# Fewer slots for the tiles of a two-layer graph network, another last pair of tiles in layer 2, and another cut of the last softmax

## The chip, the cores and the metric

The kernel runs on one core of one Trainium2 chip. A core has five engines that run their own instruction queues side by side: TensorE (PE; its weight loads are shown apart as PEld), VectorE (DVE), ScalarE (ACT), GpSimd (POOL) and SyncE (SP). Transfers between the chip's memory (DRAM) and the on-chip buffer are made by DMA engines; indirect ones, which pick rows by a list of indices, are issued by POOL, most others by SP. The metric is the device time of one execution in microseconds (us), lower is better; the number that stands for a kernel is the median of its runs.

## The reference

10,000 nodes with 768 numbers each pass through two graph attention layers with residuals. The graph has 80,000 random edges in both directions and a self loop for each node, sorted by destination; the layer adds another self loop. Cut to what matters:

```python
def gat_conv(x, edge_index, W, a_src, a_dst, bias, heads, out_ch, concat):
    xl = (x @ W).reshape(n, heads, out_ch)
    alpha_src = jnp.einsum('nhc,hc->nh', xl, a_src)
    alpha_dst = jnp.einsum('nhc,hc->nh', xl, a_dst)
    e = jax.nn.leaky_relu(alpha_src[src] + alpha_dst[dst], 0.2)
    e = jnp.exp(e - segment_max(e, dst)[dst])
    alpha = e / (segment_sum(e, dst)[dst] + 1e-16)
    out = segment_sum(xl[src] * alpha[:, :, None], dst)
    return out + bias

h = relu(layer_norm(gat_conv(x, ..., heads=4, out_ch=256))) + (x @ Wr1 + br1)
y = layer_norm(gat_conv(h, ..., heads=1, out_ch=768)) + (h @ Wr2 + br2)
return _layernorm(x + y)
```

For each node, the rows of its some 17 neighbours are fetched, weighted by a softmax over them, and added.

## The kernel before

**Sorting.** While the products `x @ W1` are made tile by tile and written to a table in DRAM (`table1`, 1033 numbers a node), `prepare` counts the neighbours of each node on the device, sorts the nodes by that count, most first, and writes for each node the list of its neighbours (`slots`). 128 nodes of the sorted order make a tile, 79 in all; a node of a tile stands on one of the 128 partitions. A tile's number of slots is the same for its 128 nodes and has to be known when the program is built. `slot_counts` (line 60 on) works it out: it takes the degree as Poisson distributed, and for tile t it looks for the smallest k for which the expected number of nodes with more than k neighbours, and a room of some standard deviations above it, is no more than t x 128. The counts of before, by sorted tile, run from 41, 27, 26, 25, 24, 24, 23 down to 11, 10, 9, 8, 1377 in all. Unused slots name a row of the table beyond the nodes, whose logit is -1e30. A comparison on the device (`fits`) sends the program to `general_path`, without slots, if a node has more neighbours than its tile has slots.

**Layer 1** (`ordered_layer1`) visits the tiles in the order `TURNS`: every second one from the smallest up to the one of 41 slots, then the others from 27 down. For each slot POOL issues one indirect DMA (`Ring.fetch`, issued by `gather`, L426) that brings one row for each of the 128 nodes into a ring of 31 slots; after the first 31, indices out of range are skipped and move nothing. ScalarE multiplies rows by their weights (L516), VectorE or PE adds them up (L523, L527, L728), and PE makes the products for the residual (L173) and for layer 2's table (L904). Near the start of the work on a tile, ScalarE copies the table row of two tiles earlier in two parts (L829).

**Layer 2** (`ordered_layer2`) fetches rows of 770 numbers into a ring of 41 slots; a tile's first slot, the nodes' own rows, is brought by SP (L455), the others by POOL, and unused slots fetch the row beyond the nodes. A slot's next row is asked for right after VectorE's step for the old one is issued, and POOL waits until VectorE and PE have both read the old one. The order of its tiles, `turns`, is made before it (line 641 on): the three smallest tiles in front, two held back for the end (`final`), and the rest mixed so that the running mean of the slots stays near the mean of all, taking the largest or the smallest of those left. For a tile t the loop issues, in this order:

- on PE the residual of tile t+1 (L1061, L1064: 34 recorded matmuls),
- on VectorE the first norm step of tile t-1: statistics of its two parts in the accumulator and of its part in PSUM (L538), then ScalarE's standard deviation (L542, L543),
- a row at a time, columns 0 to 511 on VectorE (L527), with three further norm steps of tile t-1 between the rows (L552, L554, L1074, L538, then ScalarE's L1080 and POOL's store L1082),
- from a slot called `turn` on, the logits and the softmax of tile t+1 (L489 to L507), its diagonals on ScalarE (L1018), and columns 512 to 767 of its rows on PE (L1019).

A tile of 26 slots or more (`PARTED2`: those of 41, 27 and 26) takes its softmax in two parts, with cuts from `cuts_of`: the second part's logits come three slots before the cut, its weights and PE's share one slot before it, and the sums so far are scaled by `fade`.

Of the kernel before, what the change touches and what calls it, by code (L numbers as in the profile page):

```python
# [42 lines left out]
DEGREES = 64  # L43
# [10 lines left out]
PARTED2 = 26  # L54
# [9 lines left out]
def slot_counts(n_nodes, n_edges):  # L64

    rate = max(n_edges / n_nodes - 1.0, 0.1)
    tails, term, below = [], math.exp(-rate), 0.0
    for k in range(DEGREES):
        below += term
        tails.append(max(n_nodes * (1.0 - below), 0.0))  # L70
        term *= rate / (k + 1)
    counts = []
    for t in range(-(-n_nodes // P)):
        room = t * P if t else 0.002
        k = next((k for k, m in enumerate(tails)
                  if m + 4.0 * math.sqrt(m * (1.0 - m / n_nodes)) * (t > 0) <= room), DEGREES - 3)
        counts.append(min(k + 1, DEGREES - 2))
    return counts

# [2 lines left out]
def gnn_kernel(ctx, tc, x, x_cols, src, dst, src_col, dst_col, W1, a_src1, a_dst1, b1, g1, be1, Wr1, br1,  # L82
# [9 lines left out]
    NT = -(-N // P)  # L92
    NP = NT * P
    NCH = src_col.shape[1]
    NA = dst.shape[0] // (P * P)
    CAPS = slot_counts(N, n_edges)
    SLOTS = CAPS

# [469 lines left out]
    with tc.tile_pool(name="w1", bufs=1) as w1p, tc.tile_pool(name="l1", bufs=2) as io, \  # L568
# [51 lines left out]
        for t in range(NT):  # L620
# [3 lines left out]
            for i, vec in enumerate((ad_b, as_b)):  # L624
                m = io.tile([P, C1], F32, name="scr")
# [13 lines left out]
    SLOTS, FIRST = [SLOTS[t] for t in TURNS], [FIRST[t] for t in TURNS]  # L639
    SLOTS1, FIRST1 = SLOTS, FIRST  # L640
    turns = sorted(range(NT), key=lambda t: SLOTS[t] + 2 * (t >= NT - 2))
    first, left, final = turns[:3], turns[5:], turns[3:5]
    mean, mixed = sum(SLOTS[t] for t in left) / len(left), []
    while left:
        few = sum(SLOTS[t] for t in mixed) <= mean * len(mixed)
# [1 line left out]
    turns = first + mixed + final  # L647
# [314 lines left out]
    def ordered_layer2(mem, begun):  # L962
# [4 lines left out]
        with tc.tile_pool(name="b2", bufs=1) as pool, tc.tile_pool(name="small2", bufs=2) as small, \  # L967
# [33 lines left out]
            def cuts_of(t):  # L1001

                n = SLOTS[t]
                return [0, n // 2, n] if n >= PARTED2 else [0, n]

            def weights_of(t):


                n, at, cuts = SLOTS[t], FIRST[t], cuts_of(t)
                ad = small.tile([P, H2], F32, name="ad")  # L1010
                nc.vector.tensor_add(ad, ring.slot(at)[:, C2:C2 + H2], lift)
# [83 lines left out]
            for t in range(NT):  # L1095
                n = SLOTS[t]
# [3 lines left out]
                if not ready:  # L1100
                    ahead = weights_of(t)
                    ready += itertools.islice(ahead, 2)
                es, later, cuts = dict(ready[0]), ahead, cuts_of(t)
                acc = ps_acc.tile([P, BANK], F32, name="acc")
                if not t:
# [3 lines left out]
                if t + 1 < NT:  # L1109

                    ahead = weights_of(t + 1)
                    turn = min(max(n // 3, cuts[-2] + 1, n + cuts_of(t + 1)[1] + 4 * LEAD - ring.size), n - LEAD)
# [305 lines left out]
```

## Time and profile before

| | us |
|---|---|
| median of 3 runs | 5525.66 |
| lowest and highest of them | 5516.87, 5533.84 |
| the profiled execution | 5484.34 |
| its span, first to last instruction | 5482.5 |
| mean granted TensorE clock in it | 0.944 |

In the profile, lines such as `L527 DVE SCALAR_TENSOR_TENSOR acc<-ring,e,acc` name the line of the kernel, the engine, the operation, what is written and what is read. A view by stretches gives, for each stretch of the span, its length, the busy time of each engine with the number of its instructions, the granted clock, the mean share of time in which the DMA engines were busy, and GB/s. Two groups of the page that make up most of POOL's and VectorE's work:

```profile
L426 POOL DMA_INDIRECT ring<-table,slots x2675 | 2661.1, 995 | 1515.9 <-issue 641.3
L527 DVE SCALAR_TENSOR_TENSOR acc<-ring,e,acc 128x256 f32<-128x256 f32 (+1 forms) x2574 | 1600.5, 622 | 161.4 <-PE acc L728 72.5
```

After the bar stand the busy time in us, the mean ns of one, the idle time of the engine just before such instructions, and what ended most of it.

### The profile page before, as it was taken

To read this page: it belongs to the slowest core of one execution; us is meant where nothing else is said; L and a number is where in the kernel's file an instruction comes from. 1 tells how busy PE (TensorE), PEld (TensorE's weight loads), DVE (VectorE), ACT (ScalarE), POOL (GpSimd) and SP (SyncE) were. 2 spreads that over 40 slices of the span, in tenths; PEclk is the share of its full clock that TensorE was granted. 3 is DMA by queue.
4 is the path that set the end of the run, shared out by engine and by line. 5 is a ranking of instruction groups with operands and counts; after the bars stand their busy time and mean duration, and the time that the engine had idled before them with its cause. 6 is when DMAs were issued, how large, how long until landed. Compare 5 with 4: busy or idle time off the path is not lost. (4 is left out here: it accounts for less than half of the span.)

```text
span 5482.5 us, 58273 instructions
## 1 busy us (share of the span) xinstructions
PE 4905.3 (89%) x14359; PEld 2707.8 (49%) x14359; DVE 4205.0 (77%) x7341; ACT 2959.9 (54%) x8299; POOL 3341.8 (61%) x3659
## 2 busy tenths in 40 slices
PE   8999995999999987899999997888888888888887
PEld 3444442555544443444445554555555555555554
DVE  5783343889988888888899995777777777777876
ACT  3434443778889988889888872222222222222322
POOL 2446455566667766677676644666666666666663
PEclk9999997999999998999999999989999998988898
DMA  4333636899999998999999977988898898888984
GB/s 156 121 101 90 92 94 216 312 340 363 366 369 377 379 351 291 348 360 384 372 370 363 351 268 261 327 315 309 311 323 313 305 318 304 300 300 301 315 307 168
DMA packets 474303, 1591.30 MB, mean 290 GB/s; under 512 B 118327, under 2 KB 122487, under 8 KB 473958
## 3 DMA queue, kind: packets, MB, share of 16 engines
q0 software_dynamic: 322384, 1286.62, 65.0%
q1 hardware_dynamic: 149520, 297.43, 16.2%
q10 hardware_dynamic: 2054, 3.42, 0.2%
q8 instruction: 122, 2.00, 0.1%
q14 instruction: 223, 1.83, 0.1%
HBM read 1431.80 MB, written 177.29 MB: 293 GB/s over the span
## 5 line engine op out<-in xcount | busy, mean ns | idle before, releaser
L426 POOL DMA_INDIRECT ring<-table,slots x2675 | 2661.1, 995 | 1515.9 <-issue 641.3
L516 ACT ACTIVATE ring<-ring,e 128x256 f32<-128x256 f32 x4232 | 1740.4, 507 | 87.3 <-DVE e L773 49.3
L527 DVE SCALAR_TENSOR_TENSOR acc<-ring,e,acc 128x256 f32<-128x256 f32 (+1 forms) x2574 | 1600.5, 622 | 161.4 <-PE acc L728 72.5
L523 DVE TENSOR_TENSOR acc<-acc,ring 128x1024 f32<-128x1024 f32 x781 | 961.7, 1231 | 66.9 <-ACT ring L516 12.0
L1064 PE MATMUL big<-wr,w 128*128 128x512 f32 (+1 forms) x2464 | 874.6, 499 | 129.8 <-issue 128.0
L1019 PE MATMUL big<-ring,diagonals 128*128 128x256 f32 x2754 | 743.7, 427 | 184.1 <-issue 151.2
L173 PE MATMUL big<-w,xT 128*128 128x512 f32 x1896 | 824.0, 596 | 23.0 <-DMA w<-in_W_dram 10.1
L904 PE MATMUL half<-w,hT 128*128 128x512 f32 (+1 forms) x2528 | 830.4, 486 | 0.0
L173 PE MATMUL big<-wr,xT 128*128 128x512 f32 x1896 | 830.0, 594 | 0.2 <-ACT xT L699 0.2
L1018 ACT ACTIVATE diagonals<-ident,e 128x128 f32<-128x128 f32 x1377 | 422.9, 390 | 641.9 <-PE big L1019 176.2
L1019 PEld LDWEIGHTS big<-ring,diagonals 128*128 128x128 f32 x2754 | 585.6, 216 | 343.2 <-issue 230.4
L1064 PEld LDWEIGHTS big<-wr,w 128*128 128x128 f32 x2464 | 479.9, 196 | 495.6 <-issue 465.8
L904 PEld LDWEIGHTS half<-w,hT 128*128 128x128 f32 x2528 | 477.7, 189 | 372.8 <-issue 331.7
L728 PE MATMUL acc<-ring,ident 128*128 128x512 f32 x1108 | 522.2, 618 | 107.9 <-ACT ring L516 59.8
L173 PEld LDWEIGHTS big<-w,xT 128*128 128x128 f32 x1896 | 361.4, 191 | 481.1 <-issue 463.0
L173 PEld LDWEIGHTS big<-wr,xT 128*128 128x128 f32 x1896 | 355.4, 191 | 418.2 <-issue 417.6
L542 ACT ACTIVATE sd<-mv,eps 128x1 f32<-128x1 f32 x237 | 70.0, 296 | 748.6 <-DVE mv L540 314.6
L728 PEld LDWEIGHTS acc<-ring,ident 128*128 128x128 f32 x1108 | 212.9, 196 | 372.0 <-issue 208.4
L626 DVE TENSOR_TENSOR scr<-big,ad_b 128x1024 f32<-128x1024 f32 x79 | 96.7, 1225 | 374.7 <-ACT row L623 350.9
L631 POOL TENSOR_TENSOR row<-row,none 128x1024 f32<-128x1024 f32 x79 | 187.2, 2370 | 261.4 <-ACT row L623 259.5
L629 ACT ACTIVATE scr<-scr 128x256 f32<-128x256 f32 x632 | 254.5, 404 | 120.3 <-DVE scr L626 120.3
L623 ACT COPY row<-big 128x1024 f32<-128x1024 f32 x79 | 79.7, 1009 | 312.8 <-issue 283.6
(193 smaller groups left out, 3392.8 us busy)
## 6 DMA issues: line engine op xcount, KB each, us to landing
ring<-table,slots POOLq DMA_INDIRECT x2675
table<-row SPq DMA_DIRECT2D x79, 516.0 KB
h_d<-hT SPq DMA_DIRECT2D x79, 512.0 KB
w<-h_d SPq DMA_DIRECT2D x77, 512.0 KB
table<-row SPq DMA_DIRECT2D x79, 385.0 KB
ring<-table SPq DMA_DIRECT2D x79, 385.0 KB
xT<-in_x_cols_dram SPq DMA_DIRECT2D x79, 384.0 KB
x_d<-xt SPq DMA_DIRECT2D x79, 384.0 KB
```

Source lines behind the costliest of these rows:

```text
L173: nc.tensor.matmul(p[:, c:e], aT[:, j, :], w[:, j, c:e], start=(j == 0), stop=(j == k - 1))
L426: nc.gpsimd.indirect_dma_start(out=to, out_offset=None, in_=table, in_offset=bass.IndirectOffsetOnAxis(ap=index, axis=0), **more)
L516: nc.scalar.activation(row[:, s], row[:, s], AF.Copy, scale=e[:, h:h + 1])
L523: nc.vector.tensor_add(acc[:, :c], acc[:, :c], row[:, :c])
L527: nc.vector.scalar_tensor_tensor(acc[:, s], row[:, s], e[:, h:h + 1], (acc if first is None else first)[:, s], op0=OP.mult, op1=OP.add)
L629: nc.scalar.activation(m[:, s], m[:, s], AF.Copy, accum_out=row[:, C1 + i * H1 + h:C1 + i * H1 + h + 1])
L631: nc.gpsimd.tensor_add(row[:, :C1], row[:, :C1], b1_b)
L728: nc.tensor.matmul(acc[:, c:c + BANK], ident, ring.slot(q + k)[:, c:c + BANK], start=(k == 0), stop=(k == m - 1))
L904: nc.tensor.matmul(q, hT[:, j, :], w2[:, j, c:c + q.shape[1]], start=(j == 0), stop=(j == K1 - 1))
L1018: nc.scalar.activation(diagonals[:, (k - lo) % G, :], ident, AF.Copy, scale=e[:, k - lo, :])
L1019: nc.tensor.matmul(to, diagonals[:, (k - lo) % G, :], ring.slot(at + k)[:, ON_PE2:C2], start=False, stop=(k == n - 1), skip_group_check=True)
L1064: nc.tensor.matmul(r[:, c:d], hT[:, j, :], wr2[:, j, c:d], start=False, stop=(j == K1 - 1 and d < C2), skip_group_check=True)
```

## The change

```diff
@@ slot_counts
     for t in range(-(-n_nodes // P)):
         room = t * P if t else 0.002
         k = next((k for k, m in enumerate(tails)
-                  if m + 4.0 * math.sqrt(m * (1.0 - m / n_nodes)) * (t > 0) <= room), DEGREES - 3)
+                  if m + 3.0 * math.sqrt(m * (1.0 - m / n_nodes)) * (t > 0) <= room), DEGREES - 3)
         counts.append(min(k + 1, DEGREES - 2))
@@ the order of layer 2
     turns = sorted(range(NT), key=lambda t: SLOTS[t] + 2 * (t >= NT - 2))
-    first, left, final = turns[:3], turns[5:], turns[3:5]
+    first, left, final = turns[:3], turns[3:-3] + turns[-1:], turns[-3:-1]
     mean, mixed = sum(SLOTS[t] for t in left) / len(left), []
@@ cuts_of in ordered_layer2
                 n = SLOTS[t]
-                return [0, n // 2, n] if n >= PARTED2 else [0, n]
+                return [0, n - 8 if t == NT - 1 else n // 2, n] if n >= PARTED2 else [0, n]
```

Six tiles lose one slot, by sorted place: 28 (19 to 18), 43 (17 to 16), 58 (15 to 14), 64 (14 to 13), 69 (13 to 12) and 78 (8 to 7); in layer 1's order these are the tiles 25, 61, 10, 7, 74 and 0, counted from 0. The sum is 1371. In layer 2 the tiles held back are no longer those of 11 and 9 slots but those of 26 and 27; the order becomes 7, 10, 11, 41, 11, 9, 12, 12, 25, 12, 24, 12, 13, 24, 13, 23 and so on, to 17, 18, 17, 26, 27. Before it was 8, 10, 11, 41, 12, 12, 12, 13, 13, 27, 13, 26, 13, 13, 25, 11, 24 and so on, to 18, 18, 18, 11, 9. The last tile, now of 27 slots, is cut at 19; those of 41 and 26 are still cut in the middle.

## The prediction

> **What bounds the kernel now.** I read the page first, for the share of each engine; then a view that cuts layer 2 into stretches; then the waits of VectorE in the longest of them.
>
> ```profile
> span 5482.5 us, 58273 instructions
> PE 4905.3 (89%) x14359; PEld 2707.8 (49%) x14359; DVE 4205.0 (77%) x7341; ACT 2959.9 (54%) x8299; POOL 3341.8 (61%) x3659
> PEclk9999997999999998999999999989999998988898
> DMA  4333636899999998999999977988898898888984
> POOL out_dram L1082 0%; POOLq L1365 0%
> ```
>
> The page's chain breaks off at the last store, so it names nothing; the stages have to be read one by one. The first six slices are the products and the sorting, which the change leaves alone. Slices 7 to 24 are layer 1 (DMA 9), the rest is layer 2, where nothing is full and the granted clock falls. The stretches (us, then the busy time of PE, PEld, DVE, ACT, POOL, each with its instruction count, clock, DMA share, GB/s) begin and end at VectorE's statistics of the previous tile's PSUM part (L538), the first thing it does for a new tile:
>
> ```profile
> 3382.60:3488.80 106.20, 77.20 (x252) 51.26 (x251) 69.42 (x140) 26.54 (x85) 71.26 (x75) 0.85 0.90 309
> 3488.80:3573.10 84.30, 77.64 (x257) 49.88 (x257) 80.13 (x171) 30.16 (x93) 55.45 (x59) 0.93 0.93 336
> 3573.10:5413.40 1840.30, 1545.75 (x4986) 1015.12 (x4984) 1373.72 (x2734) 521.09 (x1618) 1171.87 (x1212) 0.89 0.88 309
> 5413.40:5482.50 69.10, 43.81 (x161) 29.85 (x161) 52.70 (x104) 15.13 (x44) 3.98 (x4) 0.84 0.12 44
> ```
>
> The first row is the tiles of 8, 10, 11 and 41 rows. The second, which I call the small stretch, is five tiles of 12 and 13 rows: VectorE works 80.1 of 84.3 us. The third, the middle, is 67 tiles with 1207 rows: VectorE works 1373.7 of 1840.3 and waits 466.6 us, 7.0 a tile. The fourth, the tail, is the tiles of 18, 11 and 9 rows and the end; no gather is left in it. What VectorE waits for in the middle:
>
> ```profile
> DVE st L538 <- PE big L1064: 124.1, 15, 15.2
> DVE w L554 <- ACT sd L543: 105.5, 10, 12.0
> DVE st L538 <- remote: 99.4, 12, 11.9
> DVE w L554 <- ACT sd L542: 29.9, 3, 12.9
> ```
>
> Nearly all of it stands at the two norm steps of a tile, behind PE (in the code's order, ScalarE's standard deviation is queued behind diagonals whose buffers PE must free). So layer 2 lasts as long as VectorE's work and these waits, and the question is what the change does to each.
>
> **Rows left out, layer 1.** With the smaller room the counts at six sorted places fall by one: 19 to 18, 17 to 16, 15 to 14, 14 to 13, 13 to 12, 8 to 7; 1377 rows become 1371. In layer 1 those rows are empty slots, whose gather is told to skip out-of-range rows, so they may carry no bytes while the DMA share is 0.92 to 1.00. What a row is worth is read from tiles of equal size, by the two copies that each tile's table row takes (L829; time, busy time, copies):
>
> ```profile
> 1046.80:1097.00 50.20, 1.89 (x4) 1.00 0.92 335
> 1097.00:1175.90 78.90, 2.83 (x6) 1.00 0.92 339
> 1174.70:1285.30 110.60, 3.48 (x8) 1.00 0.94 350
> 1514.10:1603.70 89.60, 2.51 (x6) 1.00 0.98 370
> 1603.70:1634.90 31.20, 0.83 (x2) 1.00 0.98 365
> 1634.90:1728.60 93.70, 2.51 (x6) 1.00 0.99 375
> 2772.90:2886.50 113.60, 3.34 (x8) 1.00 1.00 376
> 2886.50:2967.60 81.10, 2.52 (x6) 1.00 0.98 365
> 3151.60:3225.40 73.80, 2.84 (x6) 1.00 0.94 341
> 3225.40:3248.70 23.30, 0.94 (x2) 1.00 0.94 336
> ```
>
> Per tile: 13 rows 25.1, 14 rows 26.3, 15 rows 27.65; 18 rows 29.9, 19 rows 31.2; coming down, 17 rows 28.4, 16 rows 27.0, 13 rows 24.6, 12 rows 23.3. The fifth row is the very tile of 19 whose last slot is empty: it took 31.2, as did its three neighbours with full slots. So the empty row is paid like a full one, and the time goes with the instructions. Prices: 1.2 + 1.35 + 1.3 + 1.4 + 1.3 = 6.55. The first tile saves one gather before work begins:
>
> ```profile
> 5408.63 0.95 POOL L426 DMA_INDIRECT ring<-table,slots  x1 [0.30 <-DMA ring<-table,slots]
> 5409.88 0.95 POOL L426 DMA_INDIRECT ring<-table,slots  x1 [0.31 <-issue]
> ```
>
> 0.95 + 0.30 = 1.25 us. Layer 1 gives 7.8; the lower bound is 0, if the DMA share sets the pace after all. The sorting before it issues the same instructions with lists one entry shorter: nothing. In layer 2 the first tile saves another 1.25.
>
> **Rows left out and order, layer 2.** The old order opens with 8, 10, 11, 41, then 12, 12, 12, 13, 13, and ends 18, 11, 9. The new one opens 7, 10, 11, 41, then 11, 9, 12, 12, and ends 17, 26, 27. The small stretch falls from five tiles (62 rows) to four (44). A row costs VectorE 28.35 / 38 = 0.75 us (fourth row below), so a tile with 11 instead of 12.4 rows takes 16.86 - 1.05 = 15.8, and four take 63.3: **21.0 us less**.
>
> The middle gets 69 tiles with 1205 rows in place of 67 with 1207: 26, 27 and the 13s beside them go, 34.9 rows stand in a pair of neighbours where 36.0 stood. How a pair's time goes with its rows (time, L527 busy, rows, then clock and DMA):
>
> ```profile
> 3748.60:3801.90 53.30, 26.19 (x35) 0.90 0.89 316
> 3801.90:3858.40 56.50, 28.46 (x38) 0.88 0.85 302
> 4026.20:4192.30 166.10, 83.22 (x111) 0.91 0.91 316
> 5413.40:5482.50 69.10, 28.35 (x38) 0.84 0.12 44
> 4470.90:4800.90 330.00, 161.70 (x216) 0.88 0.89 308
> 4890.60:5221.00 330.40, 161.70 (x216) 0.89 0.89 306
> 5244.70:5413.40 168.70, 80.86 (x108) 0.89 0.87 303
> ```
>
> These are pairs of 11/24, 14/24, 22/15 (three), 20/16 (six), 17/19 (six) and 18/18 (three). Two readings. By rate: the new middle has 490 rows in uneven pairs, at (53.3 + 56.5 + 166.1) / 184 = 1.50 a row; 261 in pairs like 20/15 at 330.0 / 216 = 1.53; 454 in near-equal pairs at (330.4 + 168.7) / 324 = 1.54: 735 + 399 + 699 = 1833. By slope: a pair of 38 took 3.2 more than one of 35, 1.07 a row; a tile with 0.55 fewer rows costs 27.47 - 0.59 = 26.88, times 69 = 1855. I take **1840, no change**, nearer the rates, since they are measured on pairs of the new shapes.
>
> The tail now holds 53 rows where the ring has 41 slots. The last gather goes out after row 11 of the tile of 26, so until then the pace is that of the middle; afterwards VectorE runs alone. Both tiles stand in the middle now, with the end in the third row:
>
> ```profile
> 3573.10:3611.90 38.80, 36.33 (x125) 24.06 (x123) 29.55 (x64) 11.29 (x36) 25.48 (x27) 0.96 0.87 309
> 3640.70:3672.30 31.60, 31.60 (x118) 22.93 (x118) 28.73 (x62) 10.65 (x35) 20.16 (x21) 0.94 0.86 302
> 5463.30:5482.50 19.20, 0.00 (x0) 0.00 (x0) 5.17 (x11) 2.03 (x5) 0.98 (x1) 0.50 0.10 39
> ```
>
> The tile of 26 is taken at its 31.6. The tile of 27 is taken at its VectorE work, 29.55, because its wait of 38.8 - 29.55 came with 24 gathers beside it and there will be none. With the end, 80.35 against 69.1: **11.2 us more**. If the 27 keeps its 38.8, 20.5 more.
>
> The last tile is cut at 19 rows and not at 13. Its second softmax is computed 8 rows before the end, when the last gather has long landed, so no queue waits on it; PE's last 8 rows run beside VectorE's 8 x 0.75 = 6.0. I cost this at nothing. On SP the moved tiles' own rows and residual loads are issued at the same places of the loop, two tiles ahead; POOL's queue loses 12 gathers in all and keeps its 79 stores.
>
> A rule that speaks against the small last part:
>
> ```profile
> 5390.75 10.33 PE L1019 MATMUL big<-ring,diagonals 128*128 128x256 f32 x36
> 5415.68 8.04 PE L1019 MATMUL big<-ring,diagonals 128*128 128x256 f32 x36
> ```
>
> The same 36 matmuls took 10.33 us just after a pause and 8.04 in an unbroken run. The Trainium skill, "TensorE: Matmul & The Clock Gate", section "Part 1: The HAM clock gate", says that PE runs at half clock after an idle window and needs some 3.4 us of work to get back; the two rows agree in sign. By it the sixteen matmuls of the last part, after PE's pause in the first part of the tile, would run at twice 8.04 / 36, 16 x 0.45 = 7.1, and VectorE would wait 1 us: the sum would be 18 and not 19.
>
> **The sum.** -7.8 - 1.25 - 21.0 + 0 + 11.2 = **-18.9 us** of the profiled execution's 5484.34 (span 5482.5 and 1.8 around it): 5465.4, or 0.34% less. The runs' median is 5525.66, 41 above that execution, so I carry the share over: 5525.66 x 0.9966 = 5507.
>
> **The rivals.** *The wait belongs to the boundary, not to the row.* VectorE's 7.0 us a tile then comes 69 times in the middle and not 67, +14, and its work there grows by 6 (two more tiles' fixed steps at 7 each, less the 7.8 that the split softmaxes of 26 and 27 take away): middle 1860, and the sum is +1, 5527. For it: the wait stands at the two norm steps, once a tile each. Against it: in the small stretch the boundary waits next to nothing.
>
> *Slower: the whole tile time is fixed in the middle.* Gathers, PE's signals and the norm run round a ring of 41 slots; pairs of 36, 37 and 38 rows took 55.0, 55.4 and 56.5, so perhaps a tile costs 27.47 whatever its size. Then 69 tiles take 1895, +55, and the sum is +36: 5562. It decides as soon as the middle's mean passes 27.2 us a tile (1876 in all). For it, that flat row; against, the pair of 35 at 53.3 and the 16.9 of the small tiles.
>
> *More than forecast.* If the wait falls with the rows of a pair in a straight line from 1.7 at 25 rows (small stretch) to 13.9 at 36, a pair of 34.9 waits 12.7; the middle is 1380 + 438 = 1818 and the sum is -41: 5484.
>
> *The change doesn't do what it says:* if one node has more neighbours than the smaller room, the kernel takes its general path, which this trace doesn't price and which would lie far above any range here. Counted from the reference's own inputs, the largest degrees of the six smaller tiles are 18, 16, 14, 13, 12 and 6, so each still fits, five without a slot to spare.
>
> **How the numbers follow.** The forecast with its stronger form has 0.50 (0.42 and 0.08), the boundary rival 0.31, the slower one 0.18, the general path 0.01. A measurement of this kernel tells about 0.3%, 16.6 us, from no change. So faster 0.50, within 0.30, slower 0.20. The forecast's own range is 5497 to 5521: the middle at 1833 gives -26, and layer 1 at nothing gives -11, with the middle at 1855 +4 (taken half-way, -4). The whole range goes from 5477, the stronger form less the 9 us by which the fastest run of before lay under its median, to 5546, half-way from the boundary rival to the slower one.
>
> **What would show it.** Right: layer 1's tiles at the five places shorter by 1.2 to 1.4; a small stretch near 63 after the tile of 41; 69 tiles in about 1840 us with VectorE waiting under 7 us each; about 80 us from the start of the tile of 26. Wrong: a middle above 1876, or the tile of 27 waiting at L538 for PE with no gather in flight, or at L489 for its last rows. If the middle is right and the time isn't, the tail is the next place to look; if layer 1's tiles don't shorten, DMA set their pace.

## The result, and the profile after

The changed kernel takes 5503.9 us in the median of six runs (5499.76 to 5509.41); the kernel before, measured beside it, 5529.2. The ratio is **0.9961, 95% interval 0.9949 to 0.9972**. Repeated in two later measurements it was 0.9972 (0.9962 to 0.9981) and 0.9969 (0.9958 to 0.9979). In the first of these two, one execution of the kernel before took 7509 us at a granted clock of 0.622, where the others had 0.968, and the ratios leave it out. So the change makes the kernel 0.3 to 0.4% faster, 14 to 25 us by the medians; forecast were 0.34% and 18.9 us.

The two first profiles can't be set against each other as they stand. The execution profiled of the kernel before lay 41 us under its median, that of the changed kernel lies on it:

```profile
span 5503.2 us, 58169 instructions
PE 4918.2 (89%) x14340; PEld 2709.5 (49%) x14343; DVE 4195.6 (76%) x7329; ACT 2934.8 (53%) x8273; POOL 3322.9 (60%) x3653
PEclk9999997999999998999999998898998889889888
DMA  4333636899999998999999977988898889888885
```

The busy shares and the clock are as before; POOL's instructions fall from 3659 to 3653, VectorE's work by 9 us. The view by stretches of layer 2 of the changed kernel, cut at the same events as in the prediction (us, then busy time of PE, PEld, DVE, ACT, POOL, clock, DMA share, GB/s): the tiles of 10, 11 and 41 rows (the first tile, of 7 rows now and 8 before, lies ahead of this stretch), the small stretch (11, 9, 12, 12), the middle (69 tiles, 1205 rows), the tail (26, 27 and the end).

```profile
3392.90:3498.70 105.80, 78.95 (x253) 50.77 (x251) 69.43 (x140) 26.21 (x84) 71.43 (x73) 0.82 0.91 313
3498.70:3564.20 65.50, 59.72 (x187) 37.39 (x188) 60.65 (x134) 19.85 (x62) 42.43 (x44) 0.89 0.89 312
3564.20:5418.50 1854.30, 1571.83 (x5041) 1026.08 (x5040) 1382.63 (x2750) 517.41 (x1629) 1164.74 (x1207) 0.89 0.88 306
5418.50:5503.20 84.70, 48.04 (x169) 34.65 (x167) 61.68 (x121) 19.72 (x62) 20.18 (x22) 0.80 0.34 120
```

The waits of VectorE in that middle stand at the same two norm steps as before. `remote` is what the view says where it finds no instruction that released a wait; since that step reads what PE sums in PSUM, these rows are counted here as waits behind PE too.

```profile
DVE st L538 <- remote: 154.0, 17, 15.9
DVE w L554 <- ACT sd L543: 87.6, 10, 11.4
DVE st L538 <- PE big L1064: 70.3, 9, 11.3
DVE w L554 <- ACT diagonals L1018: 22.2, 2, 11.2
```

For a fair comparison both kernels were profiled again in one measurement, on the same chip. The kernel before there (the switch between the layers with layer 2's first tile, then the four stretches):

```profile
3354.80:3406.20 51.40, 37.41 (x125) 24.07 (x124) 12.47 (x35) 6.86 (x22) 28.21 (x30) 0.90 0.85 311
3406.20:3515.30 109.10, 78.75 (x252) 53.04 (x251) 69.63 (x141) 26.50 (x85) 72.16 (x75) 0.81 0.88 298
3515.30:3603.70 88.40, 80.00 (x258) 50.62 (x257) 80.30 (x171) 30.00 (x93) 56.39 (x59) 0.93 0.92 325
3603.70:5459.10 1855.40, 1554.60 (x4986) 1022.44 (x4985) 1373.23 (x2735) 517.28 (x1619) 1169.97 (x1212) 0.88 0.88 306
5459.10:5528.10 69.00, 46.95 (x161) 31.73 (x160) 52.67 (x104) 15.02 (x44) 3.98 (x4) 0.83 0.11 41
```

And the changed kernel beside it:

```profile
3349.10:3397.80 48.70, 36.13 (x118) 22.96 (x117) 11.69 (x33) 6.56 (x21) 26.36 (x28) 0.87 0.85 308
3397.80:3505.00 107.20, 78.52 (x254) 52.17 (x254) 69.50 (x140) 26.21 (x84) 73.43 (x75) 0.82 0.90 308
3505.00:3569.20 64.20, 60.59 (x198) 37.06 (x197) 60.64 (x134) 19.85 (x62) 43.62 (x45) 0.98 0.93 334
3569.20:5422.20 1853.00, 1562.31 (x5034) 1024.15 (x5033) 1381.94 (x2751) 517.30 (x1629) 1163.44 (x1206) 0.89 0.88 306
5422.20:5505.30 83.10, 45.88 (x165) 33.70 (x164) 61.49 (x121) 19.72 (x62) 19.18 (x20) 0.79 0.32 112
```

The reader is to see three things. The middle took 1855.4 with 67 tiles and 1207 rows, and 1853.0 with 69 tiles and 1205 rows: 1.537 and 1.538 us a row, but 27.7 and 26.9 us a tile. The small stretch fell by 24.2 and the tail rose by 14.1, so the order shifts rows from one end of layer 2 to the other. And the switch between the layers is 2.7 shorter. Single profiles scatter by several us, so small differences of one pair are to be read with care; the part on the prediction sets all profiles side by side.

### The profile page after: what moved, and what is told of

Its sections match the earlier page's. It is cut to its first block, busy times and chain, and to the rows that moved or that the text cites. A ratio compares the mean times of both kernels' runs of the same rounds, so it can differ in the third digit from the quotient of the medians.

```text
span 5503.2 us, 58169 instructions
## 1 busy us (share of the span) xinstructions
PE 4918.2 (89%) x14340; PEld 2709.5 (49%) x14343; DVE 4195.6 (76%) x7329; ACT 2934.8 (53%) x8273; POOL 3322.9 (60%) x3653
## 5 line engine op out<-in xcount | busy, mean ns | idle before, releaser
L516 ACT ACTIVATE ring<-ring,e 128x256 f32<-128x256 f32 x4212 | 1726.0, 503 | 89.2 <-DVE e L773 44.8
L523 DVE TENSOR_TENSOR acc<-acc,ring 128x1024 f32<-128x1024 f32 x777 | 956.7, 1231 | 74.9 <-ACT ring L516 13.8
L173 PE MATMUL big<-w,xT 128*128 128x512 f32 x1896 | 826.2, 597 | 24.6 <-DMA w<-in_W_dram 9.5
```

The lines of the kernel that those rows point to most:

```text
L173: nc.tensor.matmul(p[:, c:e], aT[:, j, :], w[:, j, c:e], start=(j == 0), stop=(j == k - 1))
L516: nc.scalar.activation(row[:, s], row[:, s], AF.Copy, scale=e[:, h:h + 1])
L523: nc.vector.tensor_add(acc[:, :c], acc[:, :c], row[:, :c])
```

## The experiments

Three theories stood against each other, and a fourth came with the result. The row theory, the prediction's: layer 2 costs what its rows cost, and layer 1's empty slots are paid like full ones. The boundary theory: VectorE's wait comes once a tile, so two more tiles in the middle cost 14 us. The DMA theory: empty slots of layer 1 carry no bytes, so nothing is won there. The tail theory, the fourth: the gain lies in an end that no gather holds up.

Each run was timed beside the kernel before; the first four form one measurement, the next four a second, the last four a third.

**The rows alone.** Three deviations, old order:

```diff
-                  if m + 4.0 * math.sqrt(m * (1.0 - m / n_nodes)) * (t > 0) <= room), DEGREES - 3)
+                  if m + 3.0 * math.sqrt(m * (1.0 - m / n_nodes)) * (t > 0) <= room), DEGREES - 3)
```

> Room for three deviations alone: six rows fewer in each layer, the old order of layer 2 (its end 18, 11, 9), no cut of 8. Row theory (the prediction): layer 1 shorter by 7.8 us, layer 2's first tile by 1.25, and four rows or so at 1.5 us each in layer 2, together 13 to 16 us, ratio 0.9972 to 0.9976. Boundary theory (VectorE's wait comes once a tile, whatever its rows): layer 1 as before 7.8, in layer 2 only VectorE's 6 x 0.75 = 4.5, together 12, ratio 0.998; the two lie close here. DMA theory (empty slots of layer 1 carry no bytes, so nothing is won there): 5 us or less, ratio above 0.999.

Measured 0.9975 (0.9963 to 0.9987), 13 us by the medians (5507.86 against 5520.97). The DMA theory's 5 us or less is out for the whole; where the 13 us lie is not yet told.

**The order alone.** Old counts, all parted tiles cut in the middle:

```diff
-    first, left, final = turns[:3], turns[5:], turns[3:5]
+    first, left, final = turns[:3], turns[3:-3] + turns[-1:], turns[-3:-1]
```

> The new order alone, with the old counts (1377 rows), tiles of 26 and 27 rows at the end, both cut in the middle. Row theory: the small stretch and the tail take about what the old ones took, the middle is cheaper by the pairs of 26 and 27 rows: 4 to 8 us less, ratio 0.9985 to 0.9993. Boundary theory: two more tile boundaries in the middle at 7 us each less what the split softmaxes took there: 5 to 14 us more, ratio 1.001 to 1.0025. Tail theory (the whole measured gain of 22 us comes from an end that the gathers don't hold up): 0.996 to 0.997.

Measured 0.9999 (0.9988 to 1.0010): no difference that can be seen, from 7 us less to 6 more. The 4 to 8 us less that the row theory wanted did not show, and the interval holds most of that range and the smallest of the boundary theory's losses; so the time of this run doesn't decide between the two. The tail theory falls. Its middle and tail, and the same two stretches of the run with the rows alone (68 tiles with 1216 rows in the old order, then 18, 11 and 9):

```profile
3575.40:5436.70 1861.30, 1569.78 (x5042) 1023.77 (x5041) 1386.23 (x2755) 520.80 (x1634) 1166.62 (x1209) 0.89 0.88 305
5436.70:5524.60 87.90, 50.53 (x175) 36.08 (x173) 61.54 (x121) 19.84 (x62) 22.87 (x24) 0.78 0.35 126
```

```profile
3574.20:5444.30 1870.10, 1563.92 (x5041) 1026.55 (x5039) 1386.68 (x2766) 521.75 (x1634) 1174.86 (x1221) 0.89 0.88 307
5444.30:5513.10 68.80, 46.90 (x160) 31.64 (x160) 52.82 (x105) 15.03 (x44) 3.98 (x4) 0.83 0.10 39
```

The order's middle has 69 tiles and 1210 rows: 1861.3 / 1210 = 1.538 a row; the other 1870.1 / 1216 = 1.538. The boundary theory wanted the first to be dearer per row. It isn't, in these two profiles.

**The order with the cut of 8**, old counts:

```diff
-                return [0, n // 2, n] if n >= PARTED2 else [0, n]
+                return [0, n - 8 if t == NT - 1 else n // 2, n] if n >= PARTED2 else [0, n]
```

> The new order with the last tile cut 8 rows before its end, old counts. My theory: the cut costs and brings nothing, since PE's 13 or 8 rows of the second part run beside VectorE's: within 2 us of the order alone. Rival: with the cut in the middle, PE's 14 rows at half clock (14 x 0.9 = 12.5 us) end after VectorE's 14 x 0.75 = 10.5, and VectorE waits 2 us or more at the last statistics: 2 to 6 us less than the order alone.

Measured 0.9997 (0.9987 to 1.0007), 2.9 us under the order alone by the medians, within both intervals.

**Rows and order without the cut.** The edits of the first two runs together:

> Three deviations and the new order, last tile cut in the middle: the whole change but for the cut of 8. My theory: as the changed kernel within 2 us, ratio 0.996. If the parts add: the sum of the first two runs. If it is the cut that makes the order pay: 3 us or more slower than the changed kernel.

Measured 0.9980 (0.9967 to 0.9994), as the rows alone, and not the 0.996 expected. This was above the 0.9961 of the whole change, in another measurement, so the cut came into question and was taken up again below.

**The rows left out of layer 2 alone.** The lists and layer 1 keep the empty slots; layer 2 reads from them only as many as the smaller room gives, in the order that the smaller counts give (the 3.0 is the number of deviations, here an argument of `slot_counts`; the lines that follow from these are left out):

```diff
+    SLOTS2 = [slot_counts(N, n_edges, 3.0)[t] for t in TURNS]
...
-        SLOTS = [SLOTS1[t] for t in turns]
+        SLOTS = [SLOTS2[t] for t in turns]
...
-        at = [FIRST1[t] + k for t in turns for k in range(SLOTS1[t])]
+        at = [FIRST1[t] + k for t in turns for k in range(SLOTS2[t])]
```

> The six empty rows stay in the lists and in layer 1 and are left out of layer 2 alone (old order rule on the smaller counts, as in the run with the rows alone). Rows alone measured 0.9975, 13.8 us. My prices split that as 7.8 in layer 1 and 5 to 8 in layer 2: this run 0.9985 to 0.999. DMA theory (layer 1's empty rows carry no bytes and win nothing there): all of it comes from layer 2, whose empty rows do fetch a row: 0.9975 again.

Measured 0.9983 (0.9974 to 0.9993). This measurement ran under other conditions than the rest: the kernel before took 5154.5 in the median of 20 runs, not 5521. Its profile, two runs on, shows where that lies. For the question here: by the medians 9 us come from layer 2 and the switch to it, some two thirds of what the rows gave before, but the interval goes from 4 to 13 us, so this run alone leaves open whether layer 1 has a share.

**The changed kernel again**, and **the kernel before again**, in the same measurement:

> The changed kernel once more, beside the others of this call. Rows and order without the cut of 8 measured 0.998 (interval to 0.9994). If the cut costs and brings nothing, as I have it, this comes out near 0.998, within 2 us or so of that run. If it is the cut that lifts the change to the 0.9961 measured first, it comes out at 0.996 again.

Measured 0.9972 (0.9962 to 0.9981), 14.0 us by the medians: between the two values that were expected, and it decides for neither.

> The kernel before, unchanged, for a second profile: the first is of an execution 41 us under its median. Expected span 5515 to 5530. If layer 2's middle waits differ from one execution to the next, the middle is longer here than the 1840 us of the first profile by most of the 41; if it is layer 1 or the products, they are.

The expectation asked which part varies. The answer came in another form: the span was 5156.0, the products and layer 1 ended only 13 us earlier than in the first profile (the last copy of a table row began at 3319.5 and not at 3332.2), and layer 2's middle was 297 us shorter. Its small stretch, middle and tail:

```profile
3459.40:3543.50 84.10, 79.81 (x273) 52.47 (x272) 79.94 (x172) 29.79 (x93) 63.49 (x67) 0.96 1.00 379
3543.50:5086.90 1543.40, 1423.41 (x5000) 976.36 (x4999) 1371.17 (x2735) 510.74 (x1620) 1162.31 (x1203) 0.95 0.98 365
5086.90:5156.00 69.10, 35.27 (x124) 22.74 (x122) 52.64 (x105) 14.36 (x42) 10.49 (x11) 0.80 0.26 101
```

VectorE's work in the middle is the same 1371 us; its waits are 172 and not 482 (1855.4 less 1373.2, in the section on the result). The largest of them is no longer behind PE but for rows:

```profile
DVE e L489 <- DMA ring<-table,slots: 90.3, 54, 3.9
DVE w L554 <- ACT sd L543: 6.8, 5, 2.7
```

With a DMA share of 0.98 and 365 GB/s, the transfers set layer 2's pace here; under the other conditions it had 0.88 and 306 GB/s, and the waits stood behind PE. The changed kernel beside it:

```profile
3454.20:3518.40 64.20, 54.99 (x183) 35.55 (x183) 60.66 (x136) 19.54 (x62) 47.30 (x49) 0.95 0.99 365
3518.40:5063.00 1544.60, 1441.67 (x5078) 986.51 (x5077) 1379.74 (x2750) 510.83 (x1628) 1164.00 (x1201) 0.96 0.98 366
5063.00:5142.10 79.10, 36.94 (x120) 26.18 (x118) 61.37 (x122) 19.62 (x62) 24.95 (x26) 0.71 0.42 145
```

1543.4 / 1207 = 1.279 a row before, 1544.6 / 1205 = 1.282 after. The rate is another, the rule the same: the middle goes with its rows. The waits that the boundary theory counts are not there in these two profiles, so this pair says nothing about it.

**A second dose of empty rows.** The changed kernel, and the first sorted tile with 35 slots in place of 41 (the graph needs 32):

```diff
-        room = t * P if t else 0.002
+        room = t * P if t else 0.5
```

> The changed kernel with a larger tolerance for the first sorted tile, so that it has 35 slots and not 41 (the graph needs 32): six empty rows more left out in each layer, all of one tile. A dose of the same size as the change's own rows. By row prices: layer 1 took 65.9 us for the tile of 41, 1.6 a row, 9.6; layer 2 some 63.8 for 41 rows, 1.55 a row, 9.3: 19 us under the changed kernel, ratio 0.9925 to 0.995. If empty rows are worth something only where a tile's count crosses a step of PE's share: nothing, ratio as the changed kernel.

Measured 0.9914 (0.9901 to 0.9928), 5109.63 us: 31 us under the changed kernel, more than the 19 forecast. The iteration of this tile in layer 1, between the copies of table rows (L829), first of the changed kernel, then of this one:

```profile
2081.70:2146.60 64.90, 0.83 (x3) 0.84 0.76 269
```

```profile
2076.20:2133.40 57.20, 0.79 (x2) 0.88 0.84 303
```

7.7 us, or 1.3 a row. Layer 2's first stretch fell from 89.2 to 79.2, 1.7 a row. These 17.7 are near the 18.9 that the row prices gave. The DMA share of this tile in layer 1, 0.76 and 0.84, is lower than in the tiles that the change itself touches, so it doesn't tell what an empty slot costs where DMA is nearly full. The other half of the profiles' difference of 36.2 is spread: 5.1 in the other tiles of layer 1, 9.8 from the small stretch to the end though both have 1302 rows there, 2.8 in the products. Why those 9.8 went is not settled; the order of the tiles differs too, since with the smaller sum the mixing puts the tile of 25 after three small tiles and not four. It is the fastest version found; its tile has 3 slots to spare for this graph, where the general path begins.

**Without and with the cut, on one chip.** Rows and order, then the whole change, then the kernel before for its profile:

> Rows and order without the cut of 8, once more, now on the same chip as the changed kernel. My theory: the cut costs and brings nothing: within 2 us of the changed kernel. Rival: the cut brings 4 to 10 us, as 0.9961 against 0.998 in separate measurements would say.

Measured 0.9981 (0.9971 to 0.9991).

> The changed kernel, beside the run without the cut and the kernel before on one chip. By the parts as the profiles of one chip show them (layer 1 -2.7, the switch -2.5, layer 2 -9): 14 us less, ratio 0.997 to 0.9975.

Measured 0.9969 (0.9958 to 0.9979). The ratio lies just under the 0.997 to 0.9975 expected. By the medians the cut brings 7 us (2.9 with the old counts), by the intervals it may bring nothing. The timelines of the end decide for the place where it acts. The last part of the changed kernel's first profile, VectorE and then PE:

```profile
5478.03 6.30 DVE L527 SCALAR_TENSOR_TENSOR acc<-ring,e,acc 128x512 f32<-128x512 f32 x8
5485.05 0.42 DVE L538 BATCH_NORM_STATS2 st<-big 128x6 f32<-128x256 f32 x1
5478.20 5.68 PE L1019 MATMUL big<-ring,diagonals 128*128 128x256 f32 x16
```

The same without the cut:

```profile
5475.22 11.05 DVE L527 SCALAR_TENSOR_TENSOR acc<-ring,e,acc 128x512 f32<-128x512 f32 x14
5486.99 0.42 DVE L538 BATCH_NORM_STATS2 st<-big 128x6 f32<-128x256 f32 x1
5475.38 8.09 PE L1019 MATMUL big<-ring,diagonals 128*128 128x256 f32 x28
```

In both, PE's part ends before VectorE's rows do (5483.9 against 5484.3; 5483.5 against 5486.3), and VectorE comes to its last statistics without a wait. The tails were 83.1 and 79.1 us, the longer one with the cut. With the old counts it is the same: without the cut PE's 28 matmuls took 8.86 us and ended at 5502.6, VectorE's rows at 5504.7. So the end shows nothing that the cut could have won, and what is left of the 7 us is within the two intervals.

> The kernel before once more, for its profile on the same chip as the changed kernel's. By row rates: the middle's us per row within 0.01 of the changed kernel's on this chip, whatever the rate (1.53 or 1.28); layer 1 longer by 2 to 4 us; the switch to layer 2 longer by 2.5.

Its stretches stand in the section on the result: 1.537 and 1.538 a row, layer 1 from the first gather into the ring to the last copy of a table row 2462.2 against 2459.5, the switch 51.4 against 48.7. All three as expected.

**The norm steps later.** The changed kernel, where each of a tile's four norm steps on VectorE comes two rows later:

```diff
-                next(last, None)
...
-                    if k in (LEAD, 2 * LEAD, 3 * LEAD):
+                    if k in (2, LEAD + 2, 2 * LEAD + 2, 3 * LEAD + 2):
                         next(last, None)
```

> The changed kernel with each tile's four norm steps issued two rows later on VectorE: the first after the rows 0 and 1 and the others from row 5 on, where they stood before row 0 and from row 3 on. If VectorE's wait for PE at the first step (L538) sets layer 2's pace on a chip where it waits there, 1.5 us of row work now lies under each wait of 6 us or so: 60 to 100 us less there. If the pace is set by the rows (gathers, PE's late signals, the ring), the wait only moves to a later step: within 5 us. On a chip without these waits: within 5 us either way.

Measured 0.9976 (0.9963 to 0.9990), as the changed kernel's 0.9969. Its middle, and its largest waits:

```profile
3564.50:5410.60 1846.10, 1564.55 (x5037) 1024.17 (x5036) 1368.40 (x2751) 521.82 (x1624) 1172.48 (x1206) 0.89 0.88 307
```

```profile
DVE st L538 <- remote: 139.0, 18, 14.8
DVE st L538 <- PE big L1064: 115.9, 16, 12.8
DVE w L554 <- ACT sd L543: 78.9, 9, 11.3
```

1.5 us of work for each tile was moved under the wait, and the wait at L538 is as large as before: 255 us in these two rows against 224 in the changed kernel's first profile and 237 in the one of the same measurement. So VectorE's work around this wait doesn't set the pace: VectorE waits wherever the step stands. What does set it was not tried; by the rates it goes with the rows.

## Why the prediction was right, point by point

The time (5507 forecast, 5503.9 measured), the sign and the reading of layer 2's middle were right. Four terms of the sum were off: at 5521 us layer 1 gave 5.1 us less than forecast, the switch 1.5 and the small stretch 3.2 more, and the tail cost 2.9 more. That the sum came out within 1 us there is luck: the errors cancelled, and a single middle scatters by more than that. In the table, the measured values are differences of single profiles: the measurement with the kernel before at 5521 us, and the one at 5154.

| term | forecast | at 5521 | at 5154 |
|---|---|---|---|
| layer 1 | -7.8 | -2.7 | -2.7 |
| switch to layer 2 | -1.25 | -2.7 | -2.4 |
| small stretch | -21.0 | -24.2 | -19.9 |
| middle | 0 | -2.4 | +1.2 |
| tail | +11.2 | +14.1 | +10.0 |
| sum | -18.9 | -17.9 | -13.8 |

What the table leaves out is the stretch of the tiles of 10, 11 and 41, which the change doesn't touch (-1.9 and -0.3), and the products. The prediction counted the first tile, of 8 rows, into that stretch; the stretch begins with the second tile, and the first lies in the switch.

**Layer 1 was mis-sized.** The step at fault is the price of a row, taken from the mean time of tiles of equal size. Those means hold a surcharge that belongs to the step from one size to the next. The iterations of the tile that lost its fifteenth row and of the next one, before and after (time, busy, copies):

```profile
1180.00:1208.50 28.50, 0.96 (x3) 1.00 0.91 331
1208.50:1235.30 26.80, 0.82 (x2) 1.00 0.97 364
```

```profile
1175.10:1201.40 26.30, 0.95 (x3) 1.00 0.91 329
1201.40:1229.90 28.50, 0.97 (x3) 1.00 0.96 358
```

The first saves 2.2, and its neighbour, now the first of 15 rows, pays 1.7 more. Coming down it is the same: 28.6 and 26.8 became 26.9 and 27.9. A row is worth 0.5 there, not 1.35. The tile that lost its thirteenth row saved 0.8, and the two behind it paid 0.7 and 0.5 more. At two places the price held: the tile that lost its fourteenth row went from 26.2 to 24.6, and the one with the empty nineteenth slot from 31.1 to 29.9, with nothing handed on by the first. With the neighbours the five places gave some 3.5 us of the 6.55; the larger tiles between them differ by more than that from profile to profile.

The indirect transfers of layer 1 moved these bytes (packets, MB, share of 16 engines), first in the kernel before, then in the changed one, from the first gather into the ring to the last copy of a table row:

```profile
q0 software_dynamic: 204528, 737.54, 82.0%
```

```profile
q0 software_dynamic: 203664, 737.01, 82.0%
```

The 0.53 MB of difference are one row of 128 x 1033 numbers of 4 bytes, that of the first tile, which is among the first 31 slots. So the other five empty slots moved no bytes, as the DMA theory had it, and at two of the places the time was won all the same, at a DMA share of 0.93 and 0.99 before the change. At the three that gave hardly anything it was 0.91, 1.00 and 0.96, so the share doesn't tell them apart. Why they gave so little was not tried.

**The switch** gave twice the one gather that I had counted; it holds the first tile's own steps too, with one row fewer, though how the rest divides was not tried.

**The row reading of the middle held**, the point on which the forecast hung. I took no change between 1833 and 1855; the pairs of profiles gave -2.4 and +1.2. That the rates agree to 0.001 in the first pair is luck: over all profiles at 5521 us the middle took between 1.525 and 1.547 us a row, 26 us from end to end. These are the middles (the last of them has the norm steps moved):

| tiles and rows | us |
|---|---|
| 67, 1207 | 1840.3, 1855.4 |
| 68, 1216 | 1870.1 |
| 69, 1210 | 1861.3, 1858.9 |
| 69, 1205 | 1854.3, 1853.0, 1864.1, 1856.1, 1846.1 |

A straight fit through the ten, an estimate, gives 1.32 us a row and 3.8 a tile, uncertain by 0.13 and 2.3. The boundary theory's prices are 0.75 a row and, from the mean of the ten, 13.9 a tile; the row theory's are 1.54 and nothing. So the rows carry most of the middle, and a small price of a tile is not excluded. The first profile of the kernel before, at 1.525, was a quick one, which is why its 1840.3 can't be set against the 1854.3 of the changed kernel's first.

**The rivals.** *The boundary rival* asked for a middle 20 us longer and for no gain in all; the kernel was 14 to 25 us faster, the fit speaks against its prices, and moving the norm steps had no effect. The order alone, at 0.9999, doesn't exclude the mildest form of it. *The slower rival* would have needed 27.2 us a tile; the middles with 69 tiles took 26.8 to 27.0, and those with 67 and 68 tiles 27.5 to 27.7. *More than forecast* wanted the wait to fall with the rows of a pair; the rate per row didn't move. The general path wasn't taken.

**The tail** was forecast at 80.35 and took 83.1 and 79.1 (84.7 in the first profile). The step that failed is the one that gave the tile of 27 no wait because no gather would run beside it. It did wait, as the prediction named it as a sign against itself, here in the first profile:

```profile
5455.65 0.43 DVE L538 BATCH_NORM_STATS2 st<-big 128x6 f32<-128x256 f32 x1 [6.19 <-PE big L1019]
```

No gather was in flight during the wait: the DMA share was 0.01 from 5450 to 5456 us, and PE was busy all of that time. In the profile beside the kernel before the same wait was 5.44 us; at 5154 us there was none, and the tail took 79.1. The wait is more than what the tail took beyond the forecast, 4.3 and 2.7 us.

**The clock rule** was taken too far in the prediction, which has all sixteen matmuls of the last part at half clock, 7.1 us. They took 5.68 us at a mean granted clock of 0.65, more than the 3.6 of an unbroken run, and VectorE didn't wait: costing the cut at nothing was right. In three more profiles with the cut they took 5.57 to 6.69 us at a clock of 0.66 to 0.55, and VectorE's last step waited in none. The Trainium skill ("TensorE: Matmul & The Clock Gate", section "Part 1: The HAM clock gate") has only about the first 3.4 us of work after a pause at half clock; by that an estimate is 7.6 matmuls in 3.4 us and the other 8.4 in 1.9, together 5.3 us. The measured 5.57 and 5.68 lie near it, the 6.57 and 6.69 of the other two profiles nearer 7.1, which none reaches.

What is shown of the gain, then, is the rows: 13 of the 14 to 25 us by the medians. The order brings nothing by itself and nothing beside them that these intervals show: in the profile of the order alone the small stretch gains 24.2, and the middle, with three rows more, and the tail lose 5.9 and 18.9. What the cut may add, 3 to 7 us by the medians, lies within the intervals.

## What to carry to other kernels

Where work is padded to fixed sizes, count how much of it is empty before reordering anything: six of 1377 rows gave most of what three edits gave, and a run with six more left out of one tile, and the order mixed anew by that, gave twice as much. To tell whether a stage is paid by the row or by the tile, divide its time by both in several kernels that differ in tiles and hardly in rows, and look at the scatter of one kernel's profiles first; the rate that stays is the one to predict with. A wait that stays as long when the waiting step is moved isn't the bound, a sum that comes out right is looked through for errors that cancel, and the price of a size is read from tiles whose neighbours have that size too.

## What the runs showed of the hardware

The same kernel before took 5529 and twice 5521 us in three measurements and 5154 in a fourth; within each, the executions that the ratios use lie within 33 us of each other. The record gives the same chip number for the one at 5154 and the last at 5521, so whether the chip or its condition differed can't be told. Layer 1 differs little (2429.0 against 2462.2 us). Nearly all lies in layer 2's middle, where VectorE's work is the same but not its waits. The largest for the kernel before at 5521:

```profile
DVE st L538 <- remote: 145.7, 17, 17.1
DVE w L554 <- ACT sd L543: 110.6, 12, 13.0
DVE st L538 <- PE big L1064: 52.1, 7, 12.8
```

At 5154 none of its waits at the two norm steps comes to more than 6.8 us in all. There DMA moved 365 GB/s at a share of 0.98, against 306 at 0.88. What delays PE's results in the slower case stays open. The granted clock of the middle was 0.88 against 0.95, and PE was busy for 1554.6 us against 1423.4: 131 us more, where the middle took 312 us longer. Whether the lower clock is a cause or follows from the pauses was not tried.
